# Two taps of a depthwise convolution in one matmul, on the half where the channels lie twice

## The chip, the cores and the metric

The kernel runs on one core of one Trainium2 chip. The metric is the device time of the whole program in microseconds (us). Before the change it is 29334.67 us, the median of three runs (29313.72 to 29365.72).

A core has engines that run side by side: PE multiplies matrices and writes to PSUM, DVE does elementwise work and scans, ACT does activations and copies, POOL does elementwise work on SBUF, SP issues transfers. Each works through its own instructions in order and waits where another has not finished.

## The reference

Sixteen images of 48 x 48 pixels with 96 channels go through two layers. A layer normalises, projects to 192 channels, applies a depthwise 3 x 3 convolution with zero padding and a Silu, and runs a selective scan along the 2304 pixels in four directions. A gate, a side branch with a second depthwise convolution (first layer only), an output projection and a small quantised feed-forward network follow. The part that the change touches is the first convolution. For channel c and pixel (h, w), with x taken as zero outside the image:

```
xc[c, h, w] = silu( sum over i, j in 0..2 of  cw[i, j, c] * x[c, h + i - 1, w + j - 1]  +  cb[c] )
```

The scan then reads xc in rows and in columns: h = h * exp(d * A) + (d * u) * B, and y = sum over 16 states of h * C.

## The kernel before, in words

**Channels on partitions.** The 192 channels fill one tile of 128 partitions ("a", channels 0 to 127) and half of another. The second tile ("b") holds channels 128 to 191 twice, on partitions 0 to 63 and again on 64 to 127 (`DB = 128 + _P % 64`), because one copy is wanted with the image in rows and the other with it transposed: after the convolution, `done` (L383) writes the lower half to `u[1]` and the upper half, transposed, to `u[2]`.

**The convolution.** `before` (L346) projects into a padded image of 50 x 50 (`padded`, L311): for each of six quarters q of 8 rows (384 pixels; the code's NQ is 6) one matmul (L358), and one ACT copy into the inside of the image (L361). `conv` (L324) then makes nine matmuls a quarter. Tap (i, j) is a 128 x 128 diagonal matrix of that tap's weights, and its moving operand is the padded image shifted by i rows and j columns; PSUM sums the nine. The diagonals are made once at the start on DVE (L227 to L242, through one buffer `dg`), stored in DRAM, and loaded into the one `dg` buffer when a convolution begins. Every float32 matmul shows as two passes in the profile, each with its weight load.

**The scan.** `scan` (L448) takes 288 steps per image and layer. A step is one exp on ACT into PSUM (L484), a product b on POOL (L486), the scan on DVE (L518), a product hc on DVE in three steps of four and on POOL in the fourth (L520), and two matmuls that fold hc into `py` (L524). The tiles for hc have four buffers, the exp's PSUM tile two. Every 16 steps `py` is finished, copied to `yt` (L533), and begun anew by L504.

**The order of the work.** `together` (L781) runs one scan and interleaves the other image's work with it. That work is written as generators that yield a number for each piece. After scan step n, pieces are taken until their sum reaches the share below, where `total` is the sum of a fixed table:

```python
WORK = {"first": 201, "middle": 464, "final": 151}
AHEAD = 0.94
        while done < total * (n + 1) / (AHEAD * STEPS):
            done += next(other, 1e9)
```

There are 32 scans: 16 run beside a "middle" (the end of the first layer and the start of the second, 464 units), 14 beside a "final" and a "first" (352 units), one beside a first alone and one beside a final alone. Each middle and each first holds one convolution a and one convolution b (L371, L394). The first image's first stage runs before any scan, and the last image's final stage after all. Within this written order a scheduler places the instructions of each engine; the built order differs from the written one in places.

Of the kernel before, what the change touches and what calls it, by code (L numbers as in the profile page):

```python
# [11 lines left out]
F32 = mybir.dt.float32  # L12
# [4 lines left out]
ALU = mybir.AluOpType  # L17
# [3 lines left out]
HW = 48  # L21
# [7 lines left out]
PW = HW + 2  # L29
SUB = 384  # L30
# [12 lines left out]
DB = 128 + _P % 64  # L43
# [22 lines left out]
def pack_scan(pk, t, in_proj_w, conv_w, conv_b, x_proj_w, dt_proj_w, dt_proj_b, a_log, ds, out_w):  # L66

    wt = in_proj_w.T
    pk.add(t + "wxa", wt[:, :128])
    pk.add(t + "wxb", wt[:, DB])  # L70
    pk.add(t + "wza", wt[:, DI : DI + 128])
    pk.add(t + "wzb", wt[:, DI + 128 :])
    pk.add(t + "cw", np.concatenate([conv_w[:128], conv_w[DB]], 1))
    pk.add(t + "cb", np.stack([conv_b[:128], conv_b[DB]], 1))
    wbc = np.zeros((128, 3, 4, NS, 2), np.float32)
    wdt = np.zeros((128, 3, 4, DR), np.float32)
    dtw = np.zeros((4, DR, 2, 3, 128), np.float32)
    vec = np.zeros((128, 2, 3), np.float32)
    dsv = np.zeros((128, 2, 3), np.float32)
    al = np.zeros((ND, NG, 2, 3, 4, GROUPS), np.float32)  # L80
    for pair in range(2):
        for j in range(3):
            k = 2 * pair + KK[j]
            rows = x_proj_w[k, :, DD[j]]
            for kk in range(2):
                on = KK[j] == kk
                wdt[on, j, 2 * pair + kk] = rows[on, :DR]
                wbc[on, j, 2 * pair + kk, :, 0] = rows[on, DR : DR + NS]
                wbc[on, j, 2 * pair + kk, :, 1] = rows[on, DR + NS :]
                dtw[2 * pair + kk, :, pair, j, on] = dt_proj_w[k, DD[j]][on]  # L90
            vec[:, pair, j] = dt_proj_b[k, DD[j]]
            dsv[:, pair, j] = ds[k, DD[j]]

            rates = a_log[k, DD[j]].reshape(4, ND, GROUPS, NG)
            al[:, :, pair, j] = rates.transpose(1, 3, 0, 2)
    pk.add(t + "wbc", wbc)
    pk.add(t + "wdt", wdt)
    pk.add(t + "dtw", dtw.reshape(4 * DR, -1))
    pk.add(t + "dtb", vec)
    pk.add(t + "ds", dsv)  # L100
    pk.add(t + "al", al.reshape(128, -1))
    pk.add(t + "owa", out_w.T[:128])
    pk.add(t + "owb", out_w.T[128:])
# [20 lines left out]
def img(ap, w=HW):  # L124
    return ap.rearrange("p (h w) -> p h w", w=w)


def swapped(ap):

    return ap.rearrange("p (w h) -> p h w", h=HW)  # L130
# [3 lines left out]
PQ = SUB // HW  # L134
# [3 lines left out]
class Net:  # L138
    def __init__(self, ctx, tc, wpack, at, b2, ffw):
        self.tc, self.nc = tc, tc.nc  # L140
        nc = self.nc
# [17 lines left out]
        half = wpack.shape[1] // 2  # L159
# [13 lines left out]
        for t in ("l0", "l1"):  # L173
            a = self.const.tile([128, 2 * 12 * GROUPS], F32, name=t + "_a")
# [12 lines left out]
        for t, bias in (("bn1", "e1b"), ("bn2", "e2b")):  # L187
# [4 lines left out]
            b = self.const.tile([128, 3], F32, name=t + "_b")  # L192
# [7 lines left out]
        for v, name in (("g", "ong"), ("b", "onb")):  # L200
            for i, half in enumerate("ab"):
                n = (128, 64)[i]
                o = self.const.tile([n, DM], F32, name=f"ow{half}{v}")
# [21 lines left out]


        self.taps = {}  # L227
        for name, w, at in (
            ("l0a", "l0cw", 0),
            ("l0b", "l0cw", 9),  # L230
            ("l1a", "l1cw", 0),
            ("l1b", "l1cw", 9),
            ("e0", "e2w", 0),
            ("e1", "e2w", 9),
            ("e2", "e2w", 18),
        ):
            dg = self.one.tile([128, 9, 128], F32, name="dg")
            for k in range(9):
                nc.vector.tensor_scalar_mul(dg[:, k, :], self.ident, self.get(w)[:, at + k : at + k + 1])
            d = self.dram.tile([128, 9 * 128], F32, name="taps_" + name)  # L240
            nc.sync.dma_start(d, dg.rearrange("p k m -> p (k m)"))
            self.taps[name] = d  # L242
# [68 lines left out]
    def padded(self, name):  # L311
        nc = self.nc
        p = self.bigt([128, PW * PW], name)
        nc.gpsimd.memset(p[:, : PW + 1], 0.0)
        sides = p[:, PW - 1 : PW - 1 + PW * (PW - 1)].rearrange("p (r w) -> p r w", w=PW)
        nc.gpsimd.memset(sides[:, :, 0:2], 0.0)
        nc.gpsimd.memset(p[:, PW * (PW - 1) :], 0.0)
        return p

    def inside(self, p, q):  # L320

        return img(p, PW)[:, 1 + PQ * q : 1 + PQ + PQ * q, 1 : 1 + HW]

    def conv(self, p, name, done):  # L324

        nc = self.nc
        dg = self.one.tile([128, 9, 128], F32, name="dg")
        nc.sync.dma_start(dg.rearrange("p k m -> p (k m)"), self.taps[name])
        for q in range(NQ):
            o = self.pst()  # L330
            for k in range(9):
                i, j = divmod(k, 3)
                nc.tensor.matmul(  # L333
                    img(o[:, :SUB]),
                    lhsT=dg[:, k, :],
                    rhs=img(p, PW)[:, PQ * q + i : PQ * q + i + PQ, j : j + HW],
                    start=(k == 0),
                    stop=(k == 8),
                )
            yield 6  # L340
            done(q, o)
            yield 0.8

# [2 lines left out]
    def before(self, t, s, x):  # L346

        nc = self.nc
# [5 lines left out]
        for name, half in (("wxa", "a"), ("wxb", "b")):  # L354
            p = self.padded(name)
            for q in range(NQ):
                o = self.pst()
                nc.tensor.matmul(  # L358
                    o[:, :SUB], lhsT=self.get(t + name), rhs=xt[:, q * SUB : (q + 1) * SUB], start=True, stop=True
                )  # L360
                nc.scalar.copy(self.inside(p, q), img(o[:, :SUB]))  # L361
                yield 0.7
            if half == "a":
                u[0] = self.bigt([128, L], "u0")

                def done(q, o):
                    nc.scalar.activation(
                        u[0][:, q * SUB : (q + 1) * SUB], o[:, :SUB], AF.Identity, bias=cb[:, 0:1]
                    )

                yield from self.conv(p, t + half, done)  # L371
                nc.scalar.activation(u[0], u[0], AF.Silu)
                yield 1
                u[1] = self.bigt([128, L], "u1")
                nc.scalar.copy(swapped(u[1][64:]), img(u[0][64:]))
                yield 1
                u[2] = self.bigt([128, L], "u2")
                nc.scalar.copy(swapped(u[2][:64]), img(u[0][:64]))
                nc.scalar.dma_start(s["u"][0], u[0])
                yield 1  # L380
            else:

                def done(q, o):  # L383
                    nc.scalar.activation(
                        u[1][:64, q * SUB : (q + 1) * SUB], o[:64, :SUB], AF.Identity, bias=cb[:64, 1:2]
                    )
                    nc.scalar.activation(
                        swapped(u[2][64:])[:, PQ * q : PQ * q + PQ, :],
                        img(o[64:, :SUB]),
                        AF.Identity,  # L390
                        bias=cb[64:, 1:2],
                    )

                yield from self.conv(p, t + half, done)  # L394
                nc.scalar.activation(u[1][:64], u[1][:64], AF.Silu)  # L395
                nc.scalar.activation(u[2][64:], u[2][64:], AF.Silu)
                yield 1
                for j in (1, 2):
                    nc.scalar.dma_start(s["u"][j], u[j])
# [5 lines left out]
        for c in range(NCH):  # L405
            row = self.work.tile([128, CH], F32, name="row", tag="w3")
            for q in range(2):
                cs = slice(c * CH + q * SUB, c * CH + (q + 1) * SUB)
                for w, m in ((wdt, 4 * DR), (wbc, 128)):
                    o = self.pst()  # L410
# [12 lines left out]
        for pair in range(2):  # L423
            for j in range(3):
                col = 3 * pair + j
                dl = self.bigt([128, L], "dl")
                for q in range(NQ):
                    o = self.pst()
# [393 lines left out]
def packed(i):  # L822

    pk = Pack()
    for t, cw, al, ds in (
        ("l0", i["L0_conv_conv_w"].reshape(9, DI).T, "A_log", "Ds"),
        ("l1", i["L1_conv_conv_w"].reshape(DI, 9), "A_logs", "Ds"),
    ):
        g = lambda n: i[f"L{t[1]}_conv_{n}"]
        pack_scan(  # L830
            pk,
            t,
            g("in_proj_w"),
            cw,
            g("conv_b"),
            g("x_proj_w"),
            g("dt_proj_w"),
            g("dt_proj_b"),
            g(al).reshape(4, DI, NS),
            g(ds).reshape(4, DI),  # L840
            g("out_proj_w"),
        )
        pk.add(t + "b1", cols(i[f"L{t[1]}_ffn_b1"]))
# [59 lines left out]
```

## Time and profile before

| what | value |
|---|---|
| median of three runs | 29334.67 us |
| the profiled execution | 29326.56 us, span 29324.8 us |
| granted PE clock, mean | 0.898 |
| PE busy | 24033.6 us (82%), 68224 passes |
| DVE busy | 23488.3 us (80%) |
| POOL busy | 23241.6 us (79%) |
| ACT busy | 14074.7 us (48%) |
| convolution b on PE (L333, wxb) | 3456 passes, 1169.7 us |

How to read it: busy times are unions, so overlapping matmuls count once. The mean of one matmul is longer than the time from its start to the next one's start. A group of instructions has its source line, engine, operation, tiles (written <- read), and shape; after the bar stand busy time, mean time of one in ns, and the idle time of that engine just before these instructions, with what ended it. The timeline has start, length, engine, line, and how many follow each other. The scans follow each other with the same pattern: from the second on, those beside a middle take 930 to 940 us, those beside a final and a first 877 to 885 us.

### The profile page before, as it was taken

The numbers are of one execution on the slowest core, as the hardware profiler recorded it, in microseconds if no ns is written. First come the engines' busy times: TensorE is split into PE (matmuls) and PEld (weight loads), VectorE is DVE, ScalarE is ACT, GpSimd is POOL, SyncE is SP. The second block draws the span as 40 slices with busy tenths as digits, with TensorE's granted clock in tenths as the row PEclk, the third lists the DMA queues.
The fourth block names the chain that finished last, engine by engine and source line by source line (L and its number), as shares of the span: only waits on it lengthen the run. The fifth ranks groups of instructions, "written<-read, shape, count | busy, mean of one in ns | idle before, by whom it ended". The sixth has DMA issues, their size and how long they took to land. (4 is left out here: it accounts for less than half of the span.)

```text
span 29324.8 us, 227106 instructions
## 1 busy us (share of the span) xinstructions
PE 24033.6 (82%) x68224; PEld 12726.8 (43%) x68224; DVE 23488.3 (80%) x18372; ACT 14074.7 (48%) x22093; POOL 23241.6 (79%) x13238
## 2 busy tenths in 40 slices
PE   7888878888788887888788887888778888788886
PEld 3444444444444444444444444444444444344443
DVE  6877888778887788877888778887788877888777
ACT  4454444544445454444444444444444444444443
POOL 6877788778887788877888778787787877877777
PEclk8988899989999899998999989999898998989988
DMA  4444444444444444444444444444444344443443
GB/s 155 153 156 152 146 148 155 154 151 149 148 152 154 154 152 148 148 156 149 159 143 151 151 149 160 144 148 153 150 164 145 141 154 150 162 148 143 150 156 109
DMA packets 1062581, 4406.37 MB, mean 150 GB/s; under 512 B 211936, under 2 KB 211936, under 8 KB 1030368
## 3 DMA queue, kind: packets, MB, share of 16 engines
q1 hardware_dynamic: 869792, 3757.78, 36.2%
q10 hardware_dynamic: 191552, 634.06, 5.5%
q8 instruction: 536, 8.78, 0.1%
q14 instruction: 701, 5.74, 0.1%
HBM read 3500.22 MB, written 891.22 MB: 150 GB/s over the span
## 5 line engine op out<-in xcount | busy, mean ns | idle before, releaser
L486 POOL TENSOR_TENSOR b<-d,bc 128x768 f32<-128x768 f32 x9216 | 16584.7, 1819 | 4084.2 <-DVE a L518 2783.7
L524 PE MATMUL py<-hc,fold_sb 128*128 128x384 f32 x36864 | 14564.0, 540 | 3265.9 <-DVE hc L520 1991.2
L524 PEld LDWEIGHTS py<-hc,fold_sb 128*128 128x128 f32 x36864 | 7359.8, 208 | 9807.3 <-DVE hc L520 3050.8
L484 ACT ACTIVATE a<-d,l_a 128x768 f32<-128x768 f32 x9216 | 8304.2, 906 | 5248.7 <-DVE h L518 2817.0
L518 DVE TENSOR_TENSOR_SCAN a<-a,carry,b 128x768 f32<-128x768 f32 x4608 | 8252.7, 1813 | 2037.9 <-ACT a L484 1438.6
L520 DVE TENSOR_TENSOR hc<-a,bc 128x768 f32<-128x768 f32 x6912 | 6427.8, 947 | 1034.1 <-PE py L524 873.5
L520 POOL TENSOR_TENSOR hc<-h,bc 128x768 f32<-128x768 f32 x2304 | 4187.6, 1818 | 1511.8 <-DVE h L518 1115.4
L518 DVE TENSOR_TENSOR_SCAN a<-a,b 128x768 f32<-128x768 f32 x2304 | 4002.9, 1755 | 1091.6 <-ACT a L484 612.1
L522 ACT COPY carry<-a 128x1 f32<-128x1 f32 x4608 | 725.2, 158 | 5229.7 <-DVE hc L520 5210.7
L518 DVE TENSOR_TENSOR_SCAN h<-a,carry,b 128x768 f32<-128x768 f32 x1536 | 2766.9, 1801 | 484.0 <-ACT a L484 354.4
L333 PE MATMUL pst<-e,dg 128*128 128x384 f32 x5184 | 1730.3, 486 | 0.0
L430 PE MATMUL pst<-dts,wpack_sb 24*128 24x384 f32 x2304 | 1200.8, 636 | 513.9 <-ACT dl L431 434.2
L518 DVE TENSOR_TENSOR_SCAN h<-a,b 128x768 f32<-128x768 f32 x768 | 1337.2, 1741 | 303.9 <-POOL b L486 236.0
L333 PEld LDWEIGHTS pst<-e,dg 128*128 128x128 f32 x5184 | 977.2, 189 | 705.5 <-PE py L524 25.5
L333 PE MATMUL pst<-wxa,dg 128*128 128x384 f32 x3456 | 1173.3, 492 | 24.9 <-DMA dg<-taps_l0a 20.0
L442 POOL TENSOR_TENSOR du<-dl,u 128x768 f32<-128x768 f32 x576 | 1033.6, 1809 | 201.2 <-DMA dd<-du 100.4
L333 PE MATMUL pst<-wxb,dg 128*128 128x384 f32 x3456 | 1169.7, 489 | 5.6 <-issue 5.6
L431 ACT ACTIVATE dl<-pst,wpack_sb 128x384 f32<-128x384 f32 x1152 | 644.0, 577 | 1072.5 <-PE pst L430 581.4
L430 PEld LDWEIGHTS pst<-dts,wpack_sb 24*128 24x128 f32 x2304 | 446.7, 223 | 1206.6 <-ACT dl L431 661.4
L504 PE MATMUL py<-first,ident 128*128 128x384 f32 x1152 | 570.7, 629 | 484.5 <-ACT yt L533 479.6
L412 PE MATMUL pst<-u,wpack_sb 128*24 128x384 f32 (+1 forms) x2304 | 831.7, 492 | 65.2 <-ACT u L395 23.0
L333 PEld LDWEIGHTS pst<-wxa,dg 128*128 128x128 f32 x3456 | 661.5, 192 | 509.4 <-issue 44.6
(143 smaller groups left out, 15283.5 us busy)
## 6 DMA issues: line engine op xcount, KB each, us to landing
d<-dd SPq DMA_DIRECT2D x2304, 768.0 KB, 4.6
bc<-bc SPq DMA_DIRECT2D x1536, 768.0 KB, 6.0
dd<-dl ACTq DMA_DIRECT2D x192, 1152.0 KB, 4.7
dd<-du SPq DMA_DIRECT2D x576, 384.0 KB, 2.5
y<-yt ACTq DMA_DIRECT2D x576, 384.0 KB, 3.1
u<-u ACTq DMA_DIRECT2D x96, 1152.0 KB, 5.1
first<-u SPq DMA_DIRECT2D x288, 384.0 KB, 3.3
first<-y SPq DMA_DIRECT2D x288, 384.0 KB, 3.1
```

The lines of the kernel that those rows point to most:

```text
L333: nc.tensor.matmul(img(o[:, :SUB]), lhsT=dg[:, k, :], rhs=img(p, PW)[:, PQ * q + i : PQ * q + i + PQ, j : j + HW], start=(k == 0), stop=(k ...
L412: nc.tensor.matmul(o[:m, :SUB], lhsT=w[:, j, :], rhs=u[j][:, cs], start=(j == 0), stop=(j == 2))
L430: nc.tensor.matmul(o[:, :SUB], lhsT=dtw[:, col, :], rhs=dts[:, cs], start=True, stop=True)
L431: nc.scalar.activation(dl[:, cs], o[:, :SUB], AF.Identity, bias=self.get(t + "dtb")[:, col : col + 1])
L442: nc.gpsimd.tensor_tensor(du, dl[:, cs], u[j][:, cs], ALU.mult)
L484: nc.scalar.activation(a, d[:, 0, :], AF.Exp, scale=rates[:, pair, j, i, g : g + 1])
L486: nc.gpsimd.tensor_tensor(b, d[:, 1, :], bc[:, 0, :], ALU.mult)
L504: nc.tensor.matmul(py[:, q, :SUB], lhsT=self.skip[t][:, j, :] if pair == 0 else self.ident, rhs=first[:, q * SUB : (q + 1) * SUB], start=True,
L518: nc.vector.tensor_tensor_scan(way(h), way(a), way(b), start, ALU.mult, ALU.add)
L520: (nc.vector if here else nc.gpsimd).tensor_tensor(hc, h, cc, ALU.mult)
L522: nc.scalar.copy(carry[:, at : at + 1], h[:, last : last + 1])
L524: nc.tensor.matmul(py[:, q, :SUB], lhsT=self.fold[:, i, :], rhs=hc[:, q * SUB : (q + 1) * SUB], start=False, stop=((i, g) == (3, GROUPS - 1)),
```

## The change

Only tile b of the first convolution is computed in another way. Its upper half, the second copy of channels 128 to 191, is written one pixel to the left in the padded image (`inside` with x = 0). At a column j the tile then has pixel j on its lower half and pixel j + 1 on its upper half. A weight matrix with two diagonals in each half adds the two and gives the sum on both halves of the output. So the three taps of a row become one matmul of 128 rows (taps j = 0 and j = 1) and one of 64 rows (tap j = 2, from the lower half alone): six matmuls a quarter, not nine. The projection's result needs two ACT copies of 64 partitions in place of one of 128. The side columns set to zero are three wide, for every padded image. The tables of diagonals are first set to zero and, for tile b, made from a doubled identity, `twice`. The generator of convolution b yields 4 units a quarter for its matmuls, not 6; the table WORK is as it was.

```diff
-    pk.add(t + "cw", np.concatenate([conv_w[:128], conv_w[DB]], 1))
+    pairs = np.zeros((128, 6), np.float32)
+    pairs[:64, :3], pairs[64:, :3], pairs[:64, 3:] = conv_w[128:, 0::3], conv_w[128:, 1::3], conv_w[128:, 2::3]
+    pk.add(t + "cw", np.concatenate([conv_w[:128], pairs], 1))
...
+        twice = self.small.tile([128, 128], F32, name="twice")
+        for i in range(2):
+            nc.vector.tensor_tensor(
+                twice[:, 64 * i : 64 * i + 64], self.ident[:, :64], self.ident[:, 64:], ALU.add
+            )
+        for name, w, at, of, n in (
+            ("l0a", "l0cw", 0, self.ident, 9),
+            ("l0b", "l0cw", 9, twice, 6),
...
             dg = self.one.tile([128, 9, 128], F32, name="dg")
-            for k in range(9):
-                nc.vector.tensor_scalar_mul(dg[:, k, :], self.ident, self.get(w)[:, at + k : at + k + 1])
+            nc.vector.memset(dg, 0.0)
+            for k in range(n):
+                nc.vector.tensor_scalar_mul(dg[:, k, :], of, self.get(w)[:, at + k : at + k + 1])
...
-        sides = p[:, PW - 1 : PW - 1 + PW * (PW - 1)].rearrange("p (r w) -> p r w", w=PW)
-        nc.gpsimd.memset(sides[:, :, 0:2], 0.0)
+        sides = p[:, PW - 2 : PW - 2 + PW * (PW - 1)].rearrange("p (r w) -> p r w", w=PW)
+        nc.gpsimd.memset(sides[:, :, 0:3], 0.0)
...
-    def inside(self, p, q):
+    def inside(self, p, q, x=1):
...
-        return img(p, PW)[:, 1 + PQ * q : 1 + PQ + PQ * q, 1 : 1 + HW]
+        return img(p, PW)[:, 1 + PQ * q : 1 + PQ + PQ * q, x : x + HW]
...
-            for k in range(9):
-                i, j = divmod(k, 3)
+            if name[2:] == "b":
+                taps = [(k, 0, 128) for k in range(3)] + [(k, 2, 64) for k in range(3)]
+            else:
+                taps = [(*divmod(k, 3), 128) for k in range(9)]
+            for k, (i, j, n) in enumerate(taps):
                 nc.tensor.matmul(
                     img(o[:, :SUB]),
-                    lhsT=dg[:, k, :],
-                    rhs=img(p, PW)[:, PQ * q + i : PQ * q + i + PQ, j : j + HW],
+                    lhsT=dg[:n, k, :],
+                    rhs=img(p[:n], PW)[:, PQ * q + i : PQ * q + i + PQ, j : j + HW],
                     start=(k == 0),
-                    stop=(k == 8),
+                    stop=(k == len(taps) - 1),
                 )
-            yield 6
+            yield len(taps) / 1.5
             done(q, o)
             yield 0.8
...
-                nc.scalar.copy(self.inside(p, q), img(o[:, :SUB]))
+                if half == "a":
+                    nc.scalar.copy(self.inside(p, q), img(o[:, :SUB]))
+                else:
+                    nc.scalar.copy(self.inside(p[:64], q), img(o[:64, :SUB]))
+                    nc.scalar.copy(self.inside(p[64:], q, 0), img(o[64:, :SUB]))
```

More of the change, by code (lines that the diff above doesn't have):

```diff
@@ L227, in __init__ @@
         self.taps = {}
[L228 to L235, printed above, removed]
+        twice = self.small.tile([128, 128], F32, name="twice")
[6 more added lines that the diff above has]
+            ("l0b", "l0cw", 9, twice, 6),
+            ("l1a", "l1cw", 0, self.ident, 9),
+            ("l1b", "l1cw", 9, twice, 6),
+            ("e0", "e2w", 0, self.ident, 9),
+            ("e1", "e2w", 9, self.ident, 9),
+            ("e2", "e2w", 18, self.ident, 9),
         ):
             dg = self.one.tile([128, 9, 128], F32, name="dg")
-            for k in range(9):
-                nc.vector.tensor_scalar_mul(dg[:, k, :], self.ident, self.get(w)[:, at + k : at + k + 1])
+            nc.vector.memset(dg, 0.0)
+            for k in range(n):
+                nc.vector.tensor_scalar_mul(dg[:, k, :], of, self.get(w)[:, at + k : at + k + 1])
             d = self.dram.tile([128, 9 * 128], F32, name="taps_" + name)
```

## The prediction

> **What bounds the kernel now.** I read the engines' shares first, then the groups of instructions, the busy time by stretch, and the timeline around the second half of the first convolution. From the page, the engines' line for PE and the groups that matter (columns: busy us, mean ns | idle before):
>
> ```profile
> PE 24033.6 (82%) x68224; PEld 12726.8 (43%) x68224; DVE 23488.3 (80%) x18372; ACT 14074.7 (48%) x22093; POOL 23241.6 (79%) x13238
> ...
> L518 DVE TENSOR_TENSOR_SCAN a<-a,carry,b 128x768 f32<-128x768 f32 x4608 | 8252.7, 1813 | 2037.9 <-ACT a L484 1438.6
> L520 DVE TENSOR_TENSOR hc<-a,bc 128x768 f32<-128x768 f32 x6912 | 6427.8, 947 | 1034.1 <-PE py L524 873.5
> ...
> L333 PE MATMUL pst<-wxb,dg 128*128 128x384 f32 x3456 | 1169.7, 489 | 5.6 <-issue 5.6
> ```
>
> No engine is full. A scan step needs on DVE one scan (1.78 us over its four groups) and 3/4 of an hc product (0.95): 2.5 us. On PE it needs four passes (36864 / 9216). Matmuls overlap: L333 wxb takes 1169.7 / 3456 = 0.338 us a pass, not 489 ns, and 0.3225 back to back (18 passes from 2613.65 to 2619.46 below). So scan steps alone are DVE-bound, and what runs between them adds waits. The scans alone, by stretch (its length, their busy time and count, then PE clock, DMA share, GB/s; in order: convolution b in a middle, that scan's tail, convolution b in a final+first):
>
> ```profile
> 2601.00:2682.00 81.00, 48.07 (x27) 0.94 0.34 125
> 2850.00:2905.00 55.00, 34.76 (x21) 0.81 0.45 169
> 3442.00:3529.00 87.00, 48.51 (x28) 0.92 0.37 132
> ```
>
> 3.00, 2.62 and 3.11 us a step. The timeline of PE in these places, and where a 64-row tap-like matmul occurs (L593, second half of each four):
>
> ```profile
> 2228.98 1.56 PE L524 MATMUL py<-hc,fold_sb 128*128 128x384 f32 x4
> 2230.38 1.65 PE L593 MATMUL pst<-y,wpack_sb 128*128 128x384 f32 x4
> 2231.95 1.56 PE L524 MATMUL py<-hc,fold_sb 128*128 128x384 f32 x4
> ...
> 2613.65 5.97 PE L333 MATMUL pst<-wxb,dg 128*128 128x384 f32 x18
> 2619.46 5.32 PE L524 MATMUL py<-hc,fold_sb 128*128 128x384 f32 x16
> 2624.62 5.97 PE L333 MATMUL pst<-wxb,dg 128*128 128x384 f32 x18
> ...
> 3465.06 2.93 PE L524 MATMUL py<-hc,fold_sb 128*128 128x384 f32 x4 [4.33 <-POOL hc L520]
> 3467.78 7.50 PE L333 MATMUL pst<-wxb,dg 128*128 128x384 f32 x18
> ```
>
> In a middle PE has no gap: one quarter (nine taps, 18 passes) and four steps repeat every 10.97 us. In a final+first it has gaps; there the nine taps are a lump that stops the step's four passes, and DVE waits 5.63 us for an hc buffer. Last, ACT just before convolution b:
>
> ```profile
> 2586.42 4.05 ACT L378 COPY u<-u 64x2304 f32<-64x2304 f32 x1
> 2590.29 0.82 ACT L533 COPY yt<-py 128x768 f32<-128x768 f32 x1
> ...
> 2591.56 0.86 ACT L361 COPY wxb<-pst 128x384 f32<-128x384 f32 x2 [0.45 <-ACT yt L533]
> 2592.45 1.28 ACT L484 ACT_TABLE_LOAD   x1
> 2593.74 0.91 ACT L484 ACTIVATE a<-d,l_a 128x768 f32<-128x768 f32 x1
> ```
>
> Here ACT is the bound. It has worked without a pause since the Silu's table load at 2578.78; DVE waits 12.9 us for the exp at 2593.74, and two of the six wxb copies stand ahead of it.
>
> **What the Trainium skill says.** "TensorEngine Tiling (Array Packing)", Key Properties: changing the tiling mode drains the TensorE. The trace agrees: L593 with one 128-row and one 64-row matmul takes 1.57 us to the next start (2230.38 to 2231.95) and the L524 after it 1.40, together 2.97 against 8 x 0.3225 = 2.58: 0.39 us for going to 64 rows and back. "TensorE: Matmul & The Clock Gate", Part 1: the clock falls to half after about 3.4 us of idle; after the 4.33 us gap above, 18 passes take 7.50 us, not 5.97. Same page, on engine queue depths: ScalarE is strict FIFO; the exps do queue behind copies. "VectorE: DVE Perf Modes", zero memsets: one cycle per element (used below).
>
> **The change part by part.**
> Taps: 18 passes become 12 per quarter, six at 128 rows and six at 64. On PE: 18 x 0.3225 = 5.81 before, 12 x 0.3225 + 0.39 = 4.26 after; 1.55 saved a quarter, 9.3 a convolution, 297 over 32. A 64-row run with new weights for each tap isn't shown; at L593's exposed load each time it would be some 0.1 us more for four passes (0.4), and at no switch cost 3.87. I take 4.26.
> Pacing: a quarter now yields 4 + 0.8 units, not 6 + 0.8; the WORK totals stay. A middle hands out 464 / (0.94 x 288) = 1.71 units a step, a final+first 1.30. So 12 units fewer end the other work 7.0 or 9.2 steps earlier; PE gets no less per step. Middle: (4.26 + 2.8 x 1.29) / 2.8 = 2.81 us a step of PE, against 10.97 / 4 = 2.74. The saving becomes steps at the end without other work, and those are DVE-bound.
>  - Middle: before, 24 steps at 3.00 = 72.0. After, 17 at 3.00 x 2.81 / 2.74 = 3.08, 52.3, and 7 tail steps at 2.62, 18.3: 70.6. Gain 1.4; bounds -1 (the quarters' loop PE, ACT, exp gets no shorter) and +4 (two extra stalls go).
>  - Final+first: PE has room, 4.26 + 3.69 x 1.29 = 9.0 us in 3.69 steps, 2.44 a step. Before, 31 steps took 86.8 (2.80). After, if the shorter lump fits the four hc buffers, 22 at 2.55 and 9 at 2.62: 79.7. Gain 7 as the upper end, 1 if the stalls stay; I take 6.
> Copies: six L361 become twelve of 64 rows; L569 shows that 64 rows cost 470 ns against 480, and two in a row take 0.86. So +6 x 0.43 = 2.6 us of ACT per convolution, in the one stretch where ACT is late. Two extra ones delay the exp at 2593.74 by 0.86; later ones overlap with PE waits in part. I take 1.7 each (0.9 to 2.6). What is behind them: exp, so scan, so hc, so L524.
> Moved work: in a final+first the built order now puts the Silu of convolution b, the yt copy of a group's end, and the first dts and row copies into one ACT run; before, only the Silu stood there (DVE step of 9.6 us; a middle, which had dts and row there too, shows 14.8). 0 to +4.2; I take 2.
> The projections, Softplus, du and all DMA are the same in number, 6 to 13 steps earlier; they meet group ends (every 16 steps) in another phase. That is unknown, some 3 us either way for each kind of scan, the same in every repetition.
> Setup: seven memsets of 1152 columns on DVE. L165 shows 128 columns in 0.17 us; at the skill's cycle per element 1.2 each, 8.4, plus 0.3 for the doubled identity, less 1.2 for six scalings: +7.5, in the chain of tables that convolution a of the first image waits for (its dg lands at 59.3). Against it the first convolution b runs bare: -9.3. Together -2.
> Padding: 112 POOL memsets grow from 98 to 147 elements, about 0.1 us each (51 take 142 ns, 98 take 232), well ahead of the copies; 11 us of POOL hidden by its 21% idle time, all of it on the path if POOL were full.
>
> Sum: 16 middles x (-1.4 + 1.7) = +5; 14 final+firsts x (-6 + 1.7 + 2) = -32; the first scan, alone with 16 freed steps at little gain, -2; start -2. About -31, and up to twice that if the lump stalls go in middles too; I put -50 on the profiled execution's 29326.6 us and on the median 29334.67, 8 us above it: 29285.
>
> **The rivals.**
> Small gain as summed: 0.45, 29285, from 29210 to 29330. It lies across the 0.2% (59 us) that a measurement of this kernel can tell from no change.
> The lumps were the cost: every quarter stall of 2 to 5 us goes and the phase falls well: 16 x 4 + 14 x 7 - 30 x 0.9 = 135 off, 29195. For: DVE hc waits 873.5 us on L524 in all. Against: PE idles 18% already. 0.20.
> Nothing: the freed steps cost at the end what they save, within 30 us of 29335. For: the unit pacing. 0.14.
> Slower, through ACT: all six extra copies stand ahead of an awaited exp (2.6 x 32 = 83) and the Silu run costs its 4.2 (x 14 = 59), against a gain of 2 each (60): +82, 29420. It decides once the copies cost over 2.2 us a convolution and the lump stalls in final+first stay. 0.21.
>
> **How the numbers follow.** Of the first case a little over half lies under 29276 (0.25), all of the second: faster 0.45. Same: 0.19 of the first, the third, a little of the fourth: 0.34. Slower 0.21. The range, 29130 to 29420, takes the second case with its spread and the lower half of the fourth; the likeliest one's own is 29210 to 29330.
>
> **What would show it.** L333 wxb: 2304 passes, near 0.35 us each by busy time. Conv b in 17 steps of a middle at about 3.05 us, 22 of a final+first at about 2.55 with no DVE wait over 3 us on L524. L361's successors: 384 copies, the exp after Silu 0.9 to 2.6 us later. A last other matmul at step 259 and 252 of 288, not 265. Wrong if: 64-row passes start over 0.4 us apart, the tail steps cost more than 2.6, or the Softplus steps, in their new phase, stall longer than the 5 to 8 us that they show now.

## The result and the profile after

The changed kernel takes 29234.33 us (median of six runs, 29200.48 to 29248.66), the kernel before beside it 29339.03 us. The ratio is 0.9961 with a 95% interval of 0.995 to 0.9973: 0.39% faster. The profiled execution has a span of 29232.9 us, 91.9 below the 29324.8 of before. The forecast was 50 us: the right direction, and about half of what came.

The page after, first the engines' line, then groups that answer to those shown of before (lines have moved: L518 is L535, L520 is L537, L524 is L541, L333 is L346):

```profile
PE 23757.3 (81%) x67072; PEld 12460.7 (43%) x67072; DVE 23497.1 (80%) x18375; ACT 14132.9 (48%) x22283; POOL 23230.8 (79%) x13238
...
L535 DVE TENSOR_TENSOR_SCAN a<-a,carry,b 128x768 f32<-128x768 f32 x4608 | 8246.9, 1813 | 1898.8 <-ACT a L501 1422.6
L537 DVE TENSOR_TENSOR hc<-a,bc 128x768 f32<-128x768 f32 x6912 | 6423.7, 945 | 997.5 <-PE py L541 823.7
...
L346 PE MATMUL pst<-wxb,dg 128*128 128x384 f32 (+1 forms) x2304 | 823.1, 495 | 1.0
```

Convolution b is busy 346.6 us less (1169.7 - 823.1), but that group overlaps with others; PE as a whole is busy 276 us less. DVE does the same work as before. Its waits for `hc` buffers fell by 50 us. So of 276 us that PE no longer works, 92 reached the end.

The start shows the price of the taps bare, with no scan beside them. Timeline of PE in the first image, the kernel before and then the changed one:

```profile
114.72 35.41 PE L333 MATMUL pst<-wxb,dg 128*128 128x384 f32 x108
150.06 0.83 PE L412 MATMUL pst<-u,wpack_sb 128*24 128x384 f32 x2
```

```profile
64.04 36.78 PE L346 MATMUL pst<-wxa,dg 128*128 128x384 f32 x108 [23.64 <-DMA dg<-taps_l0a]
...
119.65 25.54 PE L346 MATMUL pst<-wxb,dg 128*128 128x384 f32 x72
145.12 0.83 PE L429 MATMUL pst<-u,wpack_sb 128*24 128x384 f32 x2
```

From 119.65 to 145.12 are six quarters, 4.245 us each; the forecast had 4.26. Before, the six took 35.34 us, 5.89 each.

Where the time went shows best by stretches of a scan. The bounds are the steps at which the work beside the scan changes; the means come from the start times of all 9216 scans in each trace (us, and the number of steps where it changed):

| stretch | middle, before | middle, after | final+first, before | final+first, after |
|---|---|---|---|---|
| up to Silu a | 604.8 | 604.2 | 499.9 | 500.3 |
| Silu a, projection, copies | 28.0 | 28.8 | 27.9 | 28.6 |
| convolution b | 72.2 (24) | 45.9 (17) | 86.8 (31) | 58.9 (23) |
| Silu run after it | 17.6 | 20.7 | 9.6 | 17.1 |
| projections, Softplus, du | 150.7 (44) | 159.1 (45) | 196.6 (63) | 180.1 (58) |
| no other work | 63.8 (22) | 74.8 (28) | 60.7 (22) | 93.8 (35) |
| the scan in all | 937.1 | 933.5 | 881.4 | 878.8 |

16 middles x -3.6 and 14 final+firsts x -2.6 make -94; the start gives -4.0, the first scan +6.9, the last -1.1. That is the 92 us. Two examples as the trace has them, the scans alone (columns as before: stretch, length, busy and count, clock, DMA share, GB/s; a scan that crosses a bound counts twice). The kernel before, convolution b and the Silu run, first in a middle and then in a final+first:

```profile
2603.70:2676.15 72.45, 42.71 (x24) 0.93 0.31 115
2676.16:2693.77 17.61, 3.61 (x3) 1.00 0.54 208
...
3433.61:3521.77 88.16, 53.50 (x31) 0.92 0.36 126
3521.78:3531.36 9.58, 1.81 (x2) 1.00 0.55 222
```

The changed kernel:

```profile
2601.28:2647.40 46.12, 30.26 (x17) 0.97 0.23 82
2647.41:2668.00 20.59, 3.53 (x2) 0.90 0.72 260
...
3434.06:3492.93 58.87, 39.48 (x23) 0.97 0.39 126
3492.94:3509.23 16.29, 1.80 (x2) 1.00 0.79 307
```

In a final+first the scans of convolution b now run at 2.56 us a step, close to the 2.5 that DVE itself needs. Before, DVE waited there for an `hc` buffer four times, 9.6 us in all:

```profile
DVE hc L520 <- PE py L524: 9.6, 4, 5.6
```

(in all, times, longest; us). In the changed kernel's stretch there is no such wait. But part of what the stretch gains is lost in the line after it. The timeline of ACT in that Silu run of the changed kernel:

```profile
3493.81 1.28 ACT L412 ACT_TABLE_LOAD   x1
3495.11 2.12 ACT L412 ACTIVATE u<-u 64x2304 f32<-64x2304 f32 x1
3497.26 0.80 ACT L550 COPY yt<-py 128x768 f32<-128x768 f32 x1
3498.08 2.12 ACT L413 ACTIVATE u<-u 64x2304 f32<-64x2304 f32 x1
...
3501.75 0.47 ACT L433 COPY dts<-pst 24x384 f32<-24x384 f32 x1 [1.55 <-PE pst L429]
3502.12 0.20 ACT L539 COPY carry<-a 128x1 f32<-128x1 f32 x2
3506.46 0.48 ACT L433 COPY row<-pst 128x384 f32<-128x384 f32 x1 [4.14 <-PE pst L429]
3506.95 1.28 ACT L501 ACT_TABLE_LOAD   x1
3508.25 1.73 ACT L501 ACTIVATE a<-d,l_a 128x768 f32<-128x768 f32 x2
```

The exp that DVE needs stands behind both Silus, the yt of a group end, a dts copy that waits 1.55 us and a row copy that waits 4.14 us for projections on PE. From the Silu's table load to the exp these are 14.4 us. Before, with the Silus, one carry copy and the two table loads, they were 7.1.

### The profile page after: what moved, and what is told of

Its sections match the earlier page's. It is cut to its first block, busy times and chain, and to the rows that moved or that the text cites. A ratio compares the mean times of both kernels' runs of the same rounds, so it can differ in the third digit from the quotient of the medians.

```text
span 29232.9 us, 225540 instructions
## 1 busy us (share of the span) xinstructions
PE 23757.3 (81%) x67072; PEld 12460.7 (43%) x67072; DVE 23497.1 (80%) x18375; ACT 14132.9 (48%) x22283; POOL 23230.8 (79%) x13238
## 5 line engine op out<-in xcount | busy, mean ns | idle before, releaser
L541 PE MATMUL py<-hc,fold_sb 128*128 128x384 f32 x36864 | 14633.6, 542 | 3363.8 <-DVE hc L537 2149.1
L541 PEld LDWEIGHTS py<-hc,fold_sb 128*128 128x128 f32 x36864 | 7343.3, 208 | 9998.9 <-DVE hc L537 3314.6
L535 DVE TENSOR_TENSOR_SCAN a<-a,carry,b 128x768 f32<-128x768 f32 x4608 | 8246.9, 1813 | 1898.8 <-ACT a L501 1422.6
L537 DVE TENSOR_TENSOR hc<-a,bc 128x768 f32<-128x768 f32 x6912 | 6423.7, 945 | 997.5 <-PE py L541 823.7
L537 POOL TENSOR_TENSOR hc<-h,bc 128x768 f32<-128x768 f32 x2304 | 4183.6, 1816 | 1321.4 <-DVE h L535 1056.1
L535 DVE TENSOR_TENSOR_SCAN a<-a,b 128x768 f32<-128x768 f32 x2304 | 4004.1, 1754 | 1131.0 <-ACT a L501 575.2
L535 DVE TENSOR_TENSOR_SCAN h<-a,carry,b 128x768 f32<-128x768 f32 x1536 | 2766.0, 1801 | 528.8 <-ACT a L501 334.1
L346 PE MATMUL pst<-e,dg 128*128 128x384 f32 x5184 | 1730.3, 486 | 0.0
L535 DVE TENSOR_TENSOR_SCAN h<-a,b 128x768 f32<-128x768 f32 x768 | 1336.8, 1741 | 304.0 <-ACT dl L448 141.3
L346 PEld LDWEIGHTS pst<-e,dg 128*128 128x128 f32 x5184 | 977.2, 189 | 705.5 <-PE py L541 25.5
L346 PE MATMUL pst<-wxa,dg 128*128 128x384 f32 x3456 | 1173.4, 492 | 28.5 <-DMA dg<-taps_l0a 23.6
L448 ACT ACTIVATE dl<-pst,wpack_sb 128x384 f32<-128x384 f32 x1152 | 638.7, 574 | 1019.0 <-POOL du L459 608.2
L346 PEld LDWEIGHTS pst<-wxa,dg 128*128 128x128 f32 x3456 | 661.9, 192 | 513.4 <-issue 49.1
L346 PE MATMUL pst<-wxb,dg 128*128 128x384 f32 (+1 forms) x2304 | 823.1, 495 | 1.0
```

The costliest lines, as they stand in the source:

```text
L346: nc.tensor.matmul(img(o[:, :SUB]), lhsT=dg[:n, k, :], rhs=img(p[:n], PW)[:, PQ * q + i : PQ * q + i + PQ, j : j + HW], start=(k == 0), st ...
L448: nc.scalar.activation(dl[:, cs], o[:, :SUB], AF.Identity, bias=self.get(t + "dtb")[:, col : col + 1])
L535: nc.vector.tensor_tensor_scan(way(h), way(a), way(b), start, ALU.mult, ALU.add)
L537: (nc.vector if here else nc.gpsimd).tensor_tensor(hc, h, cc, ALU.mult)
L541: nc.tensor.matmul(py[:, q, :SUB], lhsT=self.fold[:, i, :], rhs=hc[:, q * SUB : (q + 1) * SUB], start=False, stop=((i, g) == (3, GROUPS - 1)),
```

## The experiments

**The theory after the result.** The taps relieve PE and the lumps shrink (a lump is the run of tap matmuls that PE does without a fold between them); the pacing by units then moves all later work 6 to 13 steps earlier, and part of the gain is lost again. Rivals: it makes no difference where freed steps lie; the gain is only a lucky new phase; the lump's length counts and not PE's time; the copies ate it.

**1. The old pace with the new taps.** Edit to the changed kernel:

```diff
-            yield len(taps) / 1.5
+            yield 6
```

> The changed kernel, but convolution b yields 6 units a quarter as before, so the other work ends at the old step. My theory (the unit pacing hands the saved PE time to steps at the end, which DVE bounds): the 24 steps of convolution b in a middle then run at about 2.55 us (61, before 72), the 31 of a final+first at 2.56 (79, before 87), and everything after stands where it stood before: about -10 a middle and -7 a final+first, 250 us in all, 29090. Rival (it makes no difference where the saved time lands, since a freed step at the end is worth the same 2.6 us): equal to the changed kernel, 29234. Rival (the gain of the change is a lucky new phase of the later work): no better than before, 29339.

Measured: 29103.72 us, ratio to before 0.9918 (0.9906 to 0.9931). The rival of equal worth and that of a lucky phase both fall: with the other work at its old steps, the taps gain 0.82%, twice the change's 0.39%. The scans of convolution b and of the Silu run, a middle and a final+first:

```profile
2599.53:2665.08 65.55, 42.47 (x24) 0.92 0.35 127
2665.09:2683.62 18.53, 3.61 (x3) 0.91 0.50 199
...
3427.62:3509.05 81.43, 53.60 (x31) 0.96 0.40 142
3509.07:3517.98 8.91, 1.79 (x2) 1.00 0.46 193
```

In the mean a middle takes 930.9 and a final+first 871.9; convolution b falls from 72.2 to 65.7 and from 86.8 to 81.1. The forecast of 61 for the middle was too low.

**2. The new pace with the old taps.** Edit to the kernel before:

```diff
-            yield 6
+            yield 4 if name[2:] == "b" else 6
```

> The kernel before with nine taps a quarter, but yielding 4 units: only the pacing. My theory: convolution b crowds PE, 17 steps of a middle at (5.81 + 3.61) / 2.8 = 3.36 us or more and 23 of a final+first at 2.9; with the later blocks in the new place the scans cost about +7 each: 29550. Rival (phase): the new place of the later work alone is what gains, 29230 to 29300.

Measured: 29348.28 us, ratio 0.9998 (0.999 to 1.0006). Both theories miss: no loss and no gain. The scans by stretch, a middle and a final+first of this kernel, convolution b and the Silu run:

```profile
2611.15:2659.04 47.89, 30.16 (x17) 1.00 0.23 81
2659.05:2678.82 19.77, 3.53 (x2) 1.00 0.82 277
...
3442.88:3507.12 64.24, 39.39 (x23) 0.97 0.35 115
3507.13:3525.43 18.30, 1.80 (x2) 1.00 0.72 274
```

A middle takes 931.2 us, 5.9 less than before, and its 17 steps cost 2.82 us, not the 3.36 or more that PE's load was to force. A final+first takes 886.0, 4.6 more, with the Silu run at 18.3. With 2.62 us for each freed step, convolution b gains 5.9 us in a middle and 1.4 in a final+first from the pace alone; from the taps alone (run 1) it gains 6.5 and 5.6; the changed kernel, with both, has 8.0 and 6.9. So in a middle either one gets most of what both get, and in a final+first the two add up, most of it from the taps. PE shows why a middle can be crowded so. Here is this kernel around the end of a group of 16 steps (where L504 starts a new `py`), and then the kernel before:

```profile
2653.35 2.74 PE L524 MATMUL py<-hc,fold_sb 128*128 128x384 f32 x8
2655.93 2.10 PE L333 MATMUL pst<-wxb,dg 128*128 128x384 f32 x6
2657.86 1.45 PE L504 MATMUL py<-first,ident 128*128 128x384 f32 x4
```

```profile
2642.68 1.45 PE L333 MATMUL pst<-wxb,dg 128*128 128x384 f32 x4
2653.03 2.93 PE L504 MATMUL py<-first,ident 128*128 128x384 f32 x4 [8.89 <-ACT yt L533]
```

In the kernel before PE lies idle for 8.89 us in the very stretch that I had read as bound by PE; crowded, it has no such gap there. DVE runs ahead: while it does the 17 steps, PE folds 13 of them, which the four `hc` buffers allow, and what is left over of the taps and folds is done while ACT is in the Silu run. (The changed kernel still has a gap at this group end, of 5.22 us; run 1 has one of 8.59.)

**3. The copies alone.** Edit to the kernel before:

```diff
-                nc.scalar.copy(self.inside(p, q), img(o[:, :SUB]))
+                if half == "a":
+                    nc.scalar.copy(self.inside(p, q), img(o[:, :SUB]))
+                else:
+                    nc.scalar.copy(self.inside(p[:64], q), img(o[:64, :SUB]))
+                    nc.scalar.copy(self.inside(p[64:], q), img(o[64:, :SUB]))
```

> The kernel before with the wxb copy made as two of 64 partitions, nothing else: the price of the copies. My theory after the trace of the changed kernel (stretch of the projection 0.7 to 0.8 us longer): about 31 x 0.8 = +25, 29364. Rival (the copies are the price that ate the gain, all six ahead of an awaited exp): 32 x 2.6 = +83, 29422.

Measured: 29355.98 us, ratio 1.0002 (0.9994 to 1.0011). The stretch with the copies is 0.9 us longer in a middle (28.9) and 0.7 in a final+first (28.6). Six more copies of 0.47 us cost at most 0.11%; the rival of 83 us (0.28%) falls. Against this kernel, run 1 shows what the taps alone are worth, but for the setup and the wider side columns: 938.6 to 930.9 in a middle, 881.2 to 871.9 in a final+first.

**4. The third tap on 128 rows.** Edit to the changed kernel; the weights of the upper half are zero there:

```diff
-                taps = [(k, 0, 128) for k in range(3)] + [(k, 2, 64) for k in range(3)]
+                taps = [(k, 0, 128) for k in range(3)] + [(k, 2, 128) for k in range(3)]
```

> The changed kernel with tap j = 2 as a 128-row matmul whose upper 64 rows of weights are zero: no change to 64 rows and back, the same sum. 192 quarters x 0.3 to 0.39 us = 60 to 75 us less on PE. My theory (convolution b is near DVE's pace now): only the middles gain, about 6 x 0.2 a middle, 29215 to 29234. Rival (PE bounds convolution b still): 60 to 75 us off, 29165.

Measured: 29255.69 us, ratio 0.997 (0.9958 to 0.9981), against 0.9961 (0.995 to 0.9973) for the changed kernel. L346 for wxb takes 790.1 us, 33 less, and none of it reaches the end, not even the little that was forecast for the middles: convolution b takes the same 45.9 and 58.9 us. At the new pace a little less PE time in convolution b brings nothing, though nine taps in place of six cost 2.0 and 5.6 us there (run 2). The bare convolution at the start takes 23.32 us, 3.89 a quarter, against 4.245: the change to 64 rows and back costs 0.36 us.

**5. The Silu run freed, in the first stage.** Edit to the changed kernel:

```diff
                 nc.scalar.activation(u[2][64:], u[2][64:], AF.Silu)
-                yield 1
+                yield 3 if t == "l0" else 1
```

> The changed kernel (pace of 4 units), but in the first stage of layer 0 the piece after the Silu of convolution b yields 3 units, not 1: the first dts and row copies no longer stand in the same ACT run as the Silu and the group end's yt. Nothing else moves before it. My theory (half of the gain of the taps is lost where that run stops DVE for 17.1 us at step 194, before 9.6): the step falls to about 11, 14 x 6 = 84 us off, 29150 to 29170. Rival (freed steps at the end, or the phase of the Softplus blocks, are what the pace of 4 costs): within 20 us of the changed kernel, 29235 to 29255.

Measured: 29194.44 us, ratio 0.9952 (0.9939 to 0.9964); the interval overlaps that of the changed kernel, and the median lies between the two forecasts. A final+first of this kernel from Silu a to its end:

```profile
3376.68:3405.26 28.58, 8.78 (x6) 0.88 0.55 197
3405.27:3464.13 58.86, 39.48 (x23) 0.97 0.37 126
3464.14:3473.95 9.81, 1.80 (x2) 1.00 0.87 338
3473.96:3665.50 191.54, 106.74 (x60) 0.84 0.50 184
3665.51:3754.65 89.14, 58.53 (x33) 0.86 0.50 182
```

The run fell from 17.1 to 9.8 us, as expected. But the 93 steps after it rose from 273.9 to 281.0 in the mean, and the final+first from 878.8 only to 878.2. Of the 25 us between the profiled executions 13 come from the first scan alone (836.2 to 823.5). The wait went elsewhere; the theory that freeing this run returns its 7 us falls.

**6. The old taps in shorter lumps.** Edit to the kernel before, inside the loop over taps and after it:

```diff
+                if k == 4 and name[2:] == "b":
+                    yield 3
-            yield 6
+            yield 3 if name[2:] == "b" else 6
```

> The kernel before with nine taps, all of them, but convolution b's nine matmuls handed out in two lots of five and four with 3 units each: same PE work, same end, shorter lumps between the scan's matmuls. Theory of the lump (a tap run of 5.8 us exceeds what the four hc buffers cover): most of the gain of the six-tap kernel at the old pace (250 us) comes without a matmul saved, 29110 to 29200. Rival (the PE time itself is what counts): within 20 us of before, 29350.

Measured: 29323.33 us, ratio 0.9991 (0.9982 to 0.9999). Convolution b gains 2.2 us in a middle (70.0) and 3.6 in a final+first (83.2), where run 1 gained 6.5 and 5.6. But the Silu run and all after it come out 1.6 and 3.7 us longer, and little stays: a middle takes 936.5 (before 937.1), a final+first 882.1 (881.4). So shorter lumps explain some of run 1 in convolution b itself, more than half of it in a final+first, and about a tenth of its gain in all. That the rest is PE's time is the likely reading; this run does not show it by itself.

**7 and 8. Building on run 1.** The six taps at 6 units; a memset of the tables only for columns that stay unwritten; and in run 7 every convolution's matmuls handed out in two lots, in run 8 a gap of 3 units after the Silu of convolution b. Edits to the changed kernel, what both have, then run 7, then run 8:

```diff
-            nc.vector.memset(dg, 0.0)
+            if n == 6:
+                nc.vector.memset(dg[:, n:, :], 0.0)
```

```diff
-            yield len(taps) / 1.5
+                if k == len(taps) // 2 - 1:
+                    yield 3
+            yield 3
```

```diff
-            yield len(taps) / 1.5
+            yield 6
...
-                yield 1
+                yield 3
```

> Six taps at 6 units, every convolution's matmuls in two lots of 3 units each (also convolution a and the branch's), and memset of the tables only where columns stay unwritten. Lump theory: below the six-tap kernel at 6 units (29104), as the other 192 + 288 quarters have lumps of nine: some 100 to 200 us more, 29000 or less. Rival: 29104 less some 6 us of start, 29098.

> Six taps at 6 units, the memset only where needed, and 3 units after the Silu of convolution b in both layers. If dts and row behind the Silu are a cost there too (step 221 of a middle at 15.7 us): 16 x 3 + 6 off, 29050. If not: 29098.

Measured: 29031.42 us, ratio 0.9895 (0.9881 to 0.9908), and 29056.25 us, ratio 0.9904 (0.989 to 0.9917). Run 7 lies between its two forecasts, nearer to that of the lumps. Against run 1 a middle falls from 930.9 to 925.7: convolution b takes 62.5 and not 65.7, the four steps ahead of it 3.0 less. A final+first rises from 871.9 to 874.9: the stretch up to Silu a, which holds convolution a, falls from 500.1 to 495.3, but the Silu run of convolution b and all after it together take 8.8 more. So shorter lumps help where they are, in convolution b beside a middle and in convolution a beside a final, and only the middles keep the gain. In run 8 a middle falls from run 1's 930.9 to 925.6, its Silu run from 18.6 to 15.6; a final+first rises from 871.9 to 876.1, the steps after the run from 192.4 to 197.7. The gap helps in one kind of scan and costs in the other.

**9. Only the later work put back.** Edit to the changed kernel, with its crowded convolution b:

```diff
-                yield 1
+                yield 13
```

> The changed kernel at 4 units a quarter, with 13 units, not 1, after the Silu of convolution b: the 12 units that the pace took out come back as a pause there, so the later work (projections, Softplus, du) stands where it stood before, while convolution b stays crowded into 17 and 23 steps. Theory A (the pace costs because it moves the later work): back near the six-tap kernel at 6 units, 29104. Theory B (the pace costs because convolution b and its Silu run are crowded): stays at the changed kernel, 29235 to 29255; but dts and row leave the Silu run here too, which the run with a gap of 3 showed to be worth little in a final+first.

Measured: 29099.65 us, ratio 0.9917 (0.9902 to 0.9931): all of run 1's gain. Its stretches, a middle and a final+first: convolution b, the Silu run, the pause, the later work, the tail.

```profile
2586.48:2632.25 45.77, 30.27 (x17) 0.98 0.23 81
2632.26:2648.45 16.19, 3.53 (x2) 0.86 0.64 217
2648.46:2666.88 18.42, 12.40 (x7) 0.91 0.64 256
2666.89:2819.80 152.91, 78.57 (x44) 0.84 0.52 187
2819.81:2884.29 64.48, 39.05 (x22) 0.78 0.49 180
...
3414.79:3473.65 58.86, 39.48 (x23) 1.00 0.37 130
3473.66:3483.44 9.78, 1.80 (x2) 0.65 0.82 336
3483.45:3504.67 21.22, 14.22 (x8) 1.00 0.42 147
3504.68:3701.11 196.43, 112.07 (x63) 0.86 0.53 191
3701.12:3761.82 60.70, 38.87 (x22) 0.81 0.49 178
```

Set beside run 1 and the changed kernel, in the mean (us):

| stretch | middle: run 1 | changed | run 9 | final+first: run 1 | changed | run 9 |
|---|---|---|---|---|---|---|
| convolution b | 65.7 | 45.9 | 45.8 | 81.1 | 58.9 | 58.9 |
| Silu run after it | 18.6 | 20.7 | 16.1 | 8.9 | 17.1 | 9.8 |
| all after that, freed steps too | 213.0 | 233.9 | 232.4 | 253.1 | 273.9 | 278.0 |
| the scan in all | 930.9 | 933.5 | 927.9 | 871.9 | 878.8 | 875.6 |

Run 9 has convolution b exactly as the changed kernel has it and loses nothing by it, so the crowding costs nothing. The freed steps do not vanish but lie right after the Silu run, at 2.63 and 2.65 us. Against the changed kernel a middle is 5.6 us shorter and a final+first 3.2: 16 x 5.6 + 14 x 3.2 = 134, of 145 us between the two profiled executions. So theory A holds in this: half of the gain was lost because all that follows convolution b moved up against it. But by stretch the loss is not in the later work as such. In a final+first the changed kernel loses against run 1 8.1 us in the Silu run and, with 2.62 us for each freed step, nothing in the steps after it; in a middle 2.1 in the Silu run and 2.6 after it; convolution b gives 1.3 and 1.5 back. The pause of run 9 does two things, it takes dts and row out of the Silu run and puts the later work back at its old steps, and this run can't tell them apart. Run 5 does almost only the first in a final+first, and there the steps after the run took back what the run gave. Which meeting of Softplus blocks, group ends and du makes the 273.9, 278.0 and, in run 5, 281.0 stays open.

**10. The two best together.** Run 7 with the gap of run 8 at 4 units:

> Six taps at 6 units, all convolutions in two lots, memset only where needed, 4 units after the Silu of convolution b: the two best versions together. If their gains add: 29031 - 40 = 28990. If the gap only moves a wait, as in final+first before: 29031.

Measured: 28997.99 us, ratio 0.9883 (0.9867 to 0.99). A middle takes 922.9 us and a final+first 874.1, against 925.7 and 874.9 in run 7. So most of the further 40 us came. It is the fastest version here.

## Why the prediction was right or wrong

The direction was right and so was the price of the taps on PE. But the terms behind the size missed in both directions, and in a final+first their sum came out by luck. Term by term, with 2.62 us for each freed step (us a scan):

| term | middle, forecast | middle, measured | final+first, forecast | final+first, measured |
|---|---|---|---|---|
| convolution b | -1.4 | -8.0 | -6 | -6.9 |
| copies (stretch that holds them) | +1.7 | +0.8 | +1.7 | +0.7 |
| Silu run | 0 | +3.1 | +2 | +7.5 |
| later work and tail | 0, some 3 either way | +1.1 | 0, some 3 either way | -4.3 |
| up to Silu a | 0 | -0.6 | 0 | +0.5 |
| the scan in all | +0.3 | -3.6 | -2.3 | -2.6 |

**Right: the price of the taps.** The forecast had 4.26 us a quarter with one change to 64 rows and back; measured are 4.245 in the bare start, and 4.15 from 2599.64 to 2603.79 in a middle. A 64-row run with new weights for each pass costs no further exposed load: inside such a run the passes start 0.323 us apart, as at 128 rows. The cost lies at the change alone: in the bare start the first pass after it starts 0.41 us after the one before, and the next 0.43 after that.

**Right: the pacing.** The saved PE time becomes steps at the end. A last other matmul stands at steps 259 and 252 in the built order, as forecast, and the steps after it cost 2.67 and 2.68 us in the mean, near the 2.62 that the forecast had, though its own sign of being wrong was more than 2.6. Runs 1 and 9 show that the pace gives away half of what these taps can gain; with nine taps (run 2) it costs and gains nothing. The forecast had the loss as freed steps without work. They cost no more at the end than elsewhere (2.63 and 2.65 in run 9); the loss by stretch is in the Silu run and, in the middles, also behind it.

**Right: convolution b in a final+first.** Forecast were 22 steps at 2.55 and no long wait on L524; measured are 23 at 2.56 and none.

**Wrong: convolution b in a middle.** The step that failed is "In a middle PE has no gap", from which came 17 steps at 3.00 x 2.81 / 2.74 = 3.08 and a gain of 1.4 us. Measured are 2.70 and a gain of 8.0; with nine taps 2.82. Three quarters without a gap in the timeline didn't mean that the stretch was bound by PE: the same stretch holds 8.89 us of idle PE at the group end, and DVE may run up to four buffers ahead. The middles were to cost 5 us in all and gave 57. This term alone is 105 us off, more than all that lies between the summed 31 (raised to 50) and the 92 of the profile; the Silu runs, some 126 us dearer than forecast, took most of it back.

**Mis-sized: the copies.** They cost 0.8 us in the stretch that holds them, not 1.7; in run 3 the whole is within 0.11%. Two of them do delay the exp by about the forecast 0.86; the later ones do not add to it.

**Mis-sized: the Silu run.** The forecast saw from the built order that yt, dts and row would join it in a final+first, and took 2 of at most 4.2 us. It rose by 7.5. By its own figures that bound was too low: 14.8 less 9.6 is 5.2, and the yt of 0.8 comes on top. The rest are longer waits on PE: in the middle of before dts waits 0.91 us and row 3.55, here 1.55 and 4.14. In the middles the run rose too, by 3.1, which the forecast had as nothing.

**The later work: within its bound in a middle, beyond it in a final+first.** It was to be "some 3 us either way". With 7 and 8 more steps at 2.62, the later work and the tail together come out 1.1 us dearer in a middle (233.9 against 214.5 + 18.3) and 4.3 cheaper in a final+first (273.9 against 257.2 + 21.0). The forecast left the sign of this term open. With the smaller gains in the copies and in convolution b, these 4.3 cancel the 5.5 by which the Silu run was too low, and that is the luck. In a middle two steps of the later work now take 10.2 and 9.9 us in the mean, over the 5 to 8 that the forecast named as its bound. In one 10.2 us step the trace has ACT waiting 8.58 us for du on POOL; all its waits for du rise from 476.0 to 608.2 us.

**The first scan.** It was to gain 2 us and lost 6.9. What cost it is not shown; in run 5 it is 12.7 us shorter than in the changed kernel.

**The start.** -2 forecast, -4.0 measured: `dg` landed 4.7 us later (64.04, before 59.30), not 7.5, in part because the first of seven memsets lies in DVE's idle time at 1.20 us and each takes 1.02, not 1.2; the bare convolution gave 9.9.

**The rivals.** "Slower, through ACT" had its Silu run (larger than its price), but not its copies, and convolution b gained more. "The lumps were the cost" is right for convolution b in a final+first, where DVE's waits on L524 went; run 6 has more than half of that from shorter lumps with all nine taps, but keeps almost none of it over the scan. "Nothing" is what run 2 and run 3 give, each alone.

How the Trainium skill's four places fared. "TensorEngine Tiling (Array Packing)", Key Properties, on the drain at a change of tiling mode: the trace agrees, 12 passes take 4.245 us against 3.89 in run 4, which has no change; run 4 also shows that this costs the kernel nothing here. "TensorE: Matmul & The Clock Gate", Part 1, on the clock at half after idle: the trace agrees, after the 8.89 us gap shown above four passes take 2.72 us, where four back to back take 1.29. The same page on engine queue depths, on ScalarE's strict FIFO: the Silu run above agrees, the exp waits behind copies that wait for PE. "VectorE: DVE Perf Modes", on zero memsets at one cycle per element: 1.2 us was estimated from it for 1152 columns, the trace has 1.02, and the measurement decides.

## What to carry to other kernels

When one engine is relieved inside a schedule that hands out work by fixed units, what the units say decides where the saving lands: keep the old units, or put the freed ones where a pause helps, and measure both; here it was worth as much again as the change. Before crediting the saved work with a gain, run the new pace with the old work: in the middles of this kernel the pace alone got 5.9 of convolution b's 8.0 us. A run of back-to-back work on an engine doesn't make it the bound of a stretch: look for its longest idle gap in the same stretch, and for how many buffers the other engine may run ahead. A wait that is freed can come back within the next hundred steps, so judge an edit by the length of the whole period and not by the stall that it removes. And when the sum of a forecast comes out right, compare its terms one by one: two of them may have missed in opposite directions.

## What the runs showed of the hardware that was not expected

A DVE memset of 128x1152 float32 zeros took 1.018 us, 0.88 ns an element. On POOL, widening a memset of 49 rows from two to three columns (98 to 147 elements) took it from 232 to 251 ns, 0.4 ns for each further element, where the rows of 50 and 98 elements had led me to expect 0.1 us.
